# Layer 3 of a four-layer fp32 network in Strassen's form: folding, ranks and last product with seven block products, and weights turned earlier

## The chip, the cores and the metric

The kernel runs on one core of a Trainium2 chip. The metric is the device time of one execution in microseconds (us), median of several runs. A core has five engines that run their own instruction queues in order and wait for one another by semaphores: TensorE (PE, matrix products; PEld are its weight loads), VectorE (DVE), ScalarE (ACT), GpSimd (POOL) and SyncE (SP, which here issues transfers). TensorE writes its results to PSUM, eight banks of 2 KB for each of the 128 partitions; the other tiles lie in SBUF.

## What is computed

Four layers work on 1024 tokens of width 512, each adding its result to `x`. Everything is fp32. The change is in layer 3, and begins at the end of layer 2:

```python
# layer 3, first part (y = _L3_cond_ref(x)): base weights and gated low-rank experts
base = einsum('btd,od->bto', x, W)
logits = einsum('btd,ed->bte', x, Wr) + 5 * one_hot(language)
gates = softmax over the two largest logits, 0 elsewhere
y = base + 2.0 * einsum('bter,bte,eor->bto', einsum('btd,erd->bter', x, A), gates, B)
# layer 3, second part (_L3_ffn_ref(y)): 64 experts of rank 8, the best 16 gated
scores = einsum('bsr,er->bse', einsum('bsd,rd->bsr', y, Wq_w), keys)
gate = softmax over the 16 largest scores, 0 elsewhere
z = einsum('bsd,nd->bsn', y, A_w)            # 512 ranks, 8 for each expert
out = x + einsum('bsn,on->bso', z * gate, B_w) * 2.0
```

Layer 2 ends by adding to `x` a product with its weights `W2` and a gated low-rank delta.

## The kernel before

`x` lies in SBUF with the width on the partitions: four chunks of 128 (`DC`) by 1024 tokens. Tokens are worked in two halves (`g` = 0, 1) of four blocks of 128 (`HB`).

**Layers 0 to 2** fill the span up to about 1387 us; layer 2's attention is by far the longest. Several of their products are already in the form that the change brings to layer 3 (`gates_by_seven` L432, `Down` L570, `seven` L948): a product of 2x2 blocks with seven block products in place of eight, the sums of blocks made by VectorE or POOL.

**The end of layer 2** (`layer2`, L2026) runs, for each block of tokens, 16 products of 128x128 blocks into one PSUM bank (`product`, L1786, tile `h`), and leaves them there until `delta` (L1873) adds the low-rank part into the same bank, and VectorE adds the bank to `x` (L1882). Banks here carry the tags "st" (three of them), "av" (two) and "mm" (three). Blocks 0 to 2 lie in "st", 3 and 4 in "av", 5 to 7 in "mm". The routing between (L1800) is a chain on VectorE with one POOL all-reduce (L1812).

**Layer 3** (`layer3`, L2045) has a pool of eight banks of its own, which lies where the earlier banks lay. It never forms `y`. Instead it folds weights with weights:

- `weights_turned` (L1911) transposes on TensorE `base3` into `L3.W` (tile `W3p`, four banks), `wB3` into `wBT`, and `Wq3` into `wqT`; ScalarE copies each bank out (L1908).
- `fold_scores` (L1928) multiplies them with the keys: `kwp`, `fkp` (32 recorded matmuls of 64 columns) and `gkp`.
- `mids(g)` (L227, tile `midp_l`) are the products of `x` with the low-rank inputs, the router and the folded score weights; `route(g)` (L239) is a chain of some fifteen VectorE operations; `mix(g)` (L280) transposes the gated ranks (`midTp_l`) and ScalarE copies them to `midT_l` (L285).
- `fold_ranks` (L1943) makes `F` = W times A_w (tile `fp`, 16 matmuls of 512 columns) and, from `wBT`, `G` (tile `gp`).
- `scores(g)` (L1957) finishes the scores (`sc`) and picks the best 16 on VectorE: about 40 short operations.
- `ranks(g)` (L1992): for each block of tokens four matmuls of 512 columns with `F` and one with `G` into one bank (tile `z`); VectorE multiplies the bank by the gates (L2002).
- `turned(g)` (L2010) transposes the gated ranks (`zT`), ScalarE copies them to `zgT` (L2016).
- `last(g)` (L2018): 16 matmuls of 512 columns (tile `o`), VectorE adds each bank to `x` (L2023), SP sends it to HBM (L2024, 256 KB each).

In the trace each fp32 matmul of the program appears as two recorded ones.

**The order.** A planner orders each engine's instructions by the order in which the program names them and by the times at which it takes their inputs to be ready; it may put a later one ahead where an earlier one is not ready. Only those wrapped in `kept` are pinned, and layer 3's are not. VectorE's `sums_checked` (L742), for instance, is named between `turned(0)` and `last(0)` and runs at 1418 us. A tile with a tag takes the room of the last tile with that tag, once that is no longer used.

Of the kernel before, what the change touches and what calls it, by code (L numbers as in the profile page):

```python
# [10 lines left out]
F32 = mybir.dt.float32  # L11
# [6 lines left out]
P = 128  # L18
# [29 lines left out]
def forward(ctx: ExitStack, tc: tile.TileContext, a: dict, out: bass.AP):  # L48
# [615 lines left out]
    with psa:  # L664
# [53 lines left out]
        def bank(tag, shape, name):  # L718
            return ps_.tile(shape, F32, tag=tag, name=name, bufs=2 if tag == "av" else 3)

        def end_of(in_order):
            return ending(
                tc, a, out, x, ident, bias3, experts, late,
                lambda shape, name: ww.tile(shape, F32, tag="q7", name=name),
                lambda shape, name: ww.tile(shape, F32, tag="qs", name=name), chunks, mm, in_order,
            )

        y2, end = att.run(late, end_of, bank, lambda: sp.dma_start(kept, x))
# [28 lines left out]
    with tc.If(redo > 0):  # L757
        sp.dma_start(x, kept)
        y2 = attention_any(tc, a, x, ident, lens, kvrow, part, ww, wop, ypool, eps, rows, chunks, mm)
        with ExitStack() as c3:  # L760
            late = c3.enter_context(tc.tile_pool(name="late_a", bufs=1, side="right"))
            w3 = c3.enter_context(tc.tile_pool(name="w3_a", bufs=1))
            ex["sm"] = c3.enter_context(tc.tile_pool(name="sm3_a", bufs=2, side="right"))
            psp = c3.enter_context(tc.tile_pool(name="ps3_a", bufs=8, space=PSUM))

            def bank(tag, shape, name):
                return psp.tile(shape, F32, tag="mm", name=name)

            end = ending(
                tc, a, out, x, ident, bias3, experts, late,  # L770
                lambda shape, name: ww.tile(shape, F32, tag="q7", name=name),
                lambda shape, name: ww.tile(shape, F32, tag="qs", name=name), chunks, mm,
            )
            for _ in end.prepare(bank, lambda shape, name: late.tile(shape, F32, tag="oT", name=name)):
                pass
            end.load_w2()
            end.load_aw()
            end.shifted()
            end.open3(w3, ex["sm"])
            end.layer2(y2, bank)  # L780
            end.layer3(bank)
# [901 lines left out]
    return y2  # L1683


def ending(tc, a, out, x, ident, bias3, experts, early, tile_of_w2, tile_of_aw, chunks, mm, kept=lambda i: i):

# [7 lines left out]
    def half(g):  # L1697
        return slice(g * 512, (g + 1) * 512)
# [229 lines left out]
    def fold_scores(bank):  # L1928
# [11 lines left out]
            mm(ps, L3.wBT[:, o, :], kw[:, o, :], o == 0, o == DC - 1)  # L1940
        L3.GK = copied([P, NE], "gk3", ps)

    def fold_ranks(bank):  # L1943
        L3.F = L3.w3.tile([P, DC, D], F32, tag="F3", name="F3")
        for d in range(DC):
            ps = bank("mm", [P, D], f"fp_{d}")
            for o in range(DC):
                mm(ps, L3.W[:, o, d * P : (d + 1) * P], W["a"][:, o, :], o == 0, o == DC - 1)
            copied(None, None, ps, L3.F[:, d, :])
        ps = bank("mm", [P, D], "gp")  # L1950
        for o in range(DC):
            mm(ps, L3.wBT[:, o, :], W["a"][:, o, :], o == 0, o == DC - 1)
        L3.G = copied([P, D], "g3", ps)
# [35 lines left out]

    G3 = {}  # L1990

    def ranks(g, bank):  # L1992

        T = L3.steps[5]
        for i in range(HB):
            b = g * HB + i
            ps = bank("mm", [P, 512], f"z3_{b}")
            for c in range(DC):
                mm(ps, x[:, c, b * P : (b + 1) * P], L3.F[:, c, :], c == 0, False)
            mm(ps, T[g][:, i * P : (i + 1) * P], L3.G, False, True)  # L2000
            zg = L3.w3.tile([P, 512], F32, tag="zg", name=f"zg_{b}", bufs=4)
            dve.tensor_tensor(  # L2002
                zg.rearrange("p (e r) -> p e r", r=NR),
                ps.rearrange("p (e r) -> p e r", r=NR),
                gates[g][:, i, :].unsqueeze(2).to_broadcast([P, NE, NR]),
                ALU.mult,
            )
            G3[b] = zg

    def turned(g, bank):  # L2010
        for i in range(HB):
# [3 lines left out]
                pe.transpose(ps[:, c, :], G3[b][:, c * P : (c + 1) * P], ident)  # L2015
            act.copy(L3.zgT[:, :, b * P : (b + 1) * P], ps)  # L2016

    def last(g, bank):  # L2018
        for o in range(DC):
            ps = bank("mm", [P, 512], f"o3_{g}_{o}")  # L2020
            for c in range(DC):
                mm(ps, L3.Bw[:, c, o * P : (o + 1) * P], L3.zgT[:, c, half(g)], c == 0, c == DC - 1)
            dve.tensor_tensor(x[:, o, half(g)], ps, x[:, o, half(g)], ALU.add)  # L2023
            sp.dma_start(out[o * P : (o + 1) * P, half(g)], x[:, o, half(g)])  # L2024

    def layer2(y2, bank, held=lambda: None, do=range(NB)):  # L2026

# [12 lines left out]
        delta(0)  # L2040
        for b in range(HB + 1, NB):
            product(b, "mm", bank)
        delta(1)

    def layer3(bank, between=lambda: None):  # L2045
        mids, route, mix = L3.steps[:3]
# [1 line left out]
        def plain(shape, name):  # L2048
            return bank("mm", shape, name)

        weights_turned(bank)
        fold_scores(bank)
        mids(0, plain)
        route(0)
        fold_ranks(bank)
        mix(0, plain)
        scores(0, bank)
        mids(1, plain)
        route(1)
        ranks(0, bank)  # L2060
        mix(1, plain)
        scores(1, bank)
        turned(0, bank)
        between()
        last(0, bank)
        ranks(1, bank)
        turned(1, bank)
        last(1, bank)

    return SimpleNamespace(  # L2070
        prepare=prepare, load_w2=load_w2, load_aw=load_aw, turn=turn, low=low, anchors=anchors,
# [67 lines left out]
```

## Time and profile before

| | |
|---|---|
| median of three runs (1558.67 to 1561.76) | 1560.63 us |
| profiled execution | 1556.86 us, span 1555.1 us |
| TensorE busy | 1519.5 us (98% of the span) |
| VectorE / POOL / ScalarE busy | 66% / 53% / 35% |
| chain that ended last, by engine | TensorE 87%, VectorE 5%, transfers 3%, POOL 2% |
| mean granted TensorE clock | 0.995 |
| last deltas of layer 2 to the end of the span | 1431.4 to 1555.1 us |
| last addition ends; last transfer's data move | 1550.4 us; 1551.0 to 1552.5 us |

The span runs from the first to the last recorded instruction; the execution's own time has 1.8 us more. Matmuls overlap at their ends, so the duration of a group of matmuls is a little longer than the distance to the start of the next; the distance is what counts. Idle time of TensorE is printed in brackets, with what ended it.

### The profile page before, as it was taken

To read this page: it belongs to the slowest core of one execution; us is meant where nothing else is said; L and a number is where in the kernel's file an instruction comes from. 1 tells how busy PE (TensorE), PEld (TensorE's weight loads), DVE (VectorE), ACT (ScalarE), POOL (GpSimd) and SP (SyncE) were. 2 spreads that over 40 slices of the span, in tenths; PEclk is the share of its full clock that TensorE was granted. 3 is DMA by queue.
4 is the path that set the end of the run, shared out by engine and by line. 5 is a ranking of instruction groups with operands and counts; after the bars stand their busy time and mean duration, and the time that the engine had idled before them with its cause. 6 is when DMAs were issued, how large, how long until landed. Compare 5 with 4: busy or idle time off the path is not lost.

```text
span 1555.1 us, 18566 instructions
## 1 busy us (share of the span) xinstructions
PE 1519.5 (98%) x5991; PEld 928.9 (60%) x5991; DVE 1025.3 (66%) x1963; ACT 538.0 (35%) x1324; POOL 829.0 (53%) x842
## 2 busy tenths in 40 slices
PE   9999999989999999999999999999999999999998
PEld 7888886535555555556555556555555555568743
DVE  4666334477878776777877778777777878643141
ACT  1111110144445444445444445444445434321110
POOL 1341105285767777767777667777667777600000
PEclk9999999999999999999999999999999999999899
DMA  9111002154654544553454444456444435430000
GB/s 301 44 42 31 1 0 63 53 134 107 175 158 131 146 123 130 145 155 99 136 161 135 140 119 135 115 148 168 127 126 141 123 102 155 147 90 7 0 21 36
DMA packets 156682, 169.89 MB, mean 109 GB/s; under 512 B 54144, under 2 KB 127040, under 8 KB 156448
## 3 DMA queue, kind: packets, MB, share of 16 engines
q1 hardware_dynamic: 138144, 131.27, 29.7%
q0 software_dynamic: 17056, 36.49, 8.1%
q10 hardware_dynamic: 1376, 0.85, 0.2%
q8 instruction: 50, 0.82, 0.2%
q14 instruction: 56, 0.46, 0.1%
HBM read 113.89 MB, written 42.07 MB: 100 GB/s over the span
## 4 chain that ended last, share of the span: by engine, by line
PE 87%; DVE 5%; DMA 3%; POOL 2%; issue 1%; ACT 1%; SPq 0%; ACTq 0%; DVEq 0%; POOLq 0%
PE av L1177 17%; PE st L1126 16%; PE q_six L962 7%; PE g L362 7%; PE q_one L962 5%; PE q_five L962 5%; PE wo_two L962 5%; PE dn L362 5%; PE wo_six L962 3%; PE wo_one L962 3%; PE eo_l L53 2%; PE z L53 2%; PE h L1704 2%; PE o L53 2%; PE midp_l L53 1%
## 5 line engine op out<-in xcount | busy, mean ns | idle before, releaser
L905 POOL DMA_INDIRECT kn<-in_k_cache,kvrow_k x256 | 281.3, 1099 | 73.3 <-issue 66.3
L1177 PE MATMUL av<-pT,vals 128*128 128x512 f32 x640 | 300.1, 600 | 0.0
L905 POOL DMA_INDIRECT vals<-in_v_cache,kvrow_v x256 | 259.4, 1013 | 73.5 <-issue 41.8
L1130 ACT ACTIVATE pT<-st,hide 128x512 f32<-128x512 f32 x256 | 175.9, 687 | 328.7 <-PE st L1126 328.7
L1126 PE MATMUL st<-qT,kT 128*128 128x512 f32 x512 | 235.9, 593 | 2.9 <-DMA qT<-turned_new 2.8
L1051 POOL TENSOR_TENSOR vq<-q,txq 128x256 f32<-128x256 f32 x128 | 118.3, 954 | 174.8 <-ACT sqq L1035 122.5
L1177 PEld LDWEIGHTS av<-pT,vals 128*128 128x128 f32 x640 | 119.5, 191 | 144.9 <-issue 143.0
L1126 PEld LDWEIGHTS st<-qT,kT 128*128 128x128 f32 x512 | 96.7, 190 | 111.9 <-issue 105.2
L1146 DVE TENSOR_TENSOR part<-pT 128x512 f32<-128x512 f32 x128 | 88.4, 693 | 80.4 <-ACT pT L1130 80.4
L962 PE MATMUL q_one<-q,x 128*128 128x384 f32 x256 | 93.0, 486 | 0.0
L1162 DVE RECIPROCAL rr<-sum 128x256 f32<-128x256 f32 x32 | 56.2, 1756 | 41.3 <-PE sum L1155 41.3
L1035 ACT ACTIVATE sqq<-q 128x128 f32<-128x128 f32 x256 | 79.3, 310 | 11.3 <-DVE q L1011 4.6
L962 PEld LDWEIGHTS q_one<-q,x 128*128 128x128 f32 x256 | 48.5, 190 | 39.8 <-issue 14.3
L962 PE MATMUL q_six<-q_s,xs_all 128*128 128x384 f32 x192 | 69.8, 486 | 0.0
L962 PE MATMUL wo_one<-o,oT 128*128 128x256 f32 x256 | 65.7, 379 | 0.0
L1126 PE MATMUL st<-qT,kTn 128*128 128x512 f32 x128 | 65.4, 592 | 0.0
L1215 POOL TENSOR_TENSOR y<-y,uo 128x512 f32<-128x512 f32 x32 | 41.3, 1290 | 43.3 <-DVE y L1207 42.8
L1016 ACT COPY q<-q_one 128x256 f32<-128x256 f32 x32 | 11.9, 372 | 148.7 <-PE q_one L962 148.7
L962 PE MATMUL wo_two<-o_s,os 128*128 128x256 f32 x256 | 60.6, 380 | 2.5 <-DVE os L921 2.3
L1130 ACT ACTIVATE pT<-st,rs 128x512 f32<-128x512 f32 x64 | 44.0, 687 | 38.4 <-PE st L1126 38.3
L962 PEld LDWEIGHTS wo_one<-o,oT 128*128 128x128 f32 x256 | 48.6, 190 | 13.4 <-PE st L1126 0.4
L362 PE MATMUL g<-xs,ws 128*128 128x256 f32 (+1 forms) x240 | 55.2, 379 | 1.4 <-POOL ws L429 1.4
(396 smaller groups left out, 2693.5 us busy)
## 6 DMA issues: line engine op xcount, KB each, us to landing
turned_new<-qkt SPq DMA_DIRECT2D x126, 160.0 KB
turned_cached<-kt SPq DMA_DIRECT2D x128, 128.0 KB
kT<-turned_cached SPq DMA_DIRECT2D x32, 512.0 KB
qT<-turned_new SPq DMA_DIRECT2D x32, 512.0 KB
R<-R SPq DMA_DIRECT2D x96, 128.0 KB
q<-in_WqT SPq DMA_DIRECT2D x8, 1024.0 KB
o<-in_WoT SPq DMA_DIRECT2D x8, 1024.0 KB
kn<-in_k_cache,kvrow_k POOLq DMA_INDIRECT x256, 2.9
```

The lines of the kernel that those rows point to most:

```text
L53: pe.matmul(o, lhsT, rhs, start=start, stop=stop)
L362: pe.matmul(o, lhsT, rhs, start=start, stop=stop, skip_group_check=True)
L905: kept(pool.indirect_dma_start(out=d[:, c, :], out_offset=None, in_=kc if what == "k" else vc, in_offset=bass.IndirectOffsetOnAxis(ap=kvro ...
L962: kept(pe.matmul(o, l[:, c, :], r[:, c, :], start=start and c == 0, stop=c == 1, skip_group_check=True))
L1035: kept(act.activation(sq, S[n][m][:, j, i, :], AF.Square, accum_out=S[n]["ssq"][:, j, col : col + 1]))
L1051: kept(pool.tensor_tensor(to, t[:, b, :, hi : hi + 64], wx[:, b, lo : lo + 64].unsqueeze(2).to_broadcast(list(to.shape)), ALU.mult,))
L1126: kept(pe.matmul(ps, s["kT"][:, c, 4 * j : 4 * j + 4, :] if c < 4 else s["kn"][:, j], s["qT"][:, :, REP * j : REP * (j + 1), :].rearrange( ...
L1130: kept(act.activation(pT[:, c, :, :].rearrange("p i t -> p (i t)"), ps, AF.Exp, **(dict(bias=hide[:, b, c : c + 1]) if c < 4 else dict(bia ...
L1146: kept(dve.tensor_tensor(o, l, r, ALU.add))
L1162: kept(dve.reciprocal(r, S[n]["sum"]))
L1177: kept(pe.matmul(ps, v[:, c, :], pT[:, c, :, :].rearrange("p i t -> p (i t)"), start=c == 0, stop=c == NC - 1, skip_group_check=True,))
L1215: kept(pool.tensor_tensor(t, t, u.unsqueeze(1).to_broadcast([P, 2, HW]), ALU.add))
```

## The change

A block product C = A B with A and B cut into 2x2 blocks is made from seven products of blocks: P1 = a11 b11, then a12 b21, s1 t1, s2 t2, s3 t3, s4 b22 and a22 t4, where s1 to s4 are sums and differences of A's blocks and t1 to t4 of B's. One set (`Seven`) makes four outputs of 128 rows by 256 columns, in two banks, `even` and `odd`, of two outputs each. ScalarE copies P1 out; VectorE makes two further partial sums (`u`, and `p1` in two steps) while the matmuls go on, and the outputs but the first are a bank half plus one of these.

- `fold_ranks` makes `F` in two sets, `ranks` each half in two, `last` each half in two: ten sets. `G` is made in a function of its own, `fold_last`, named after `mix(0)`.
- POOL makes the sums of the left operands (`left_sums`): of `Bw` and `W` once, of `x` for each half. VectorE makes those of the right operands (`right_sums`): of `AwT`, `F` and `zgT`. Their tiles take the room of tags "y", "os", "o7", "q7" and "qs", whose earlier tiles are used no more by then.
- A gate is now multiplied onto a quarter of a pair of blocks at a time; outputs go out in 16 transfers of 128 KB.
- `weights_turned` is named in `layer2` ahead of the last deltas, `fold_scores` after them, both with "st" banks.
- In `layer3`, `turned(0)` stands before `scores(1)`; the first set of `last(0)` stands before `ranks(1)` and the second after it; in the second half both P1 are made before the other products.

The core of the diff:

```diff
+    def left_sums(a11, a12, a21, a22, t, by):
+        s1, s2, s3, s4 = (t[:, k] for k in range(4))
+        for o, l, r, op in (
+            (s1, a21, a22, ALU.add), (s2, s1, a11, ALU.subtract),
+            (s3, a11, a21, ALU.subtract), (s4, a12, s2, ALU.subtract),
+        ):
+            by.tensor_tensor(o, l, r, op)
+        return a11, a12, a22, s1, s2, s3, s4
+
+    def right_sums(b11, b12, b21, b22, t):
+        t1, t2, t3, t4 = (t[:, k] for k in range(4))
+        for o, l, r in ((t1, b12, b11), (t2, b22, t1), (t3, b22, b12), (t4, b21, t2)):
+            dve.tensor_tensor(o, l, r, ALU.subtract)
+        return b11, b21, b22, t1, t2, t3, t4
...
+    class Seven:
+        def __init__(self, name, bank, A, B):
+            self.A, self.B = A, B
+            self.even, self.odd = (bank("mm", [P, 2, 256], f"{name}_{i}") for i in range(2))
+            self.p1, self.u = (
+                L3.w3.tile([P, 256], F32, tag=f"seven_{n}", name=f"{n}_{name}", bufs=2) for n in ("p", "u")
+            )
+            self.c = {(0, 0): (self.even[:, 0], None), (0, 1): (self.odd[:, 1], self.u),
+                      (1, 0): (self.even[:, 1], self.u), (1, 1): (self.odd[:, 0], self.p1)}
+        def into(self, o, l, r, start=False):
+            for c in range(2):
+                mmq(o, l[:, c, :], r[:, c, :], start and c == 0, False)
+        def begin(self):
+            self.into(self.even[:, 0], self.A[0], self.B[0], True)
+            act.copy(self.p1, self.even[:, 0])
+        def go_on(self):
...
+            self.into(odd[:, 1], s1, t1, True)
+            self.into(odd[:, 0], s2, t2)
+            dve.tensor_tensor(u, odd[:, 0], p1, ALU.add)
+            dve.tensor_tensor(p1, odd[:, 1], p1, ALU.add)
+            self.into(even[:, 1], s3, t3)
+            dve.tensor_tensor(p1, even[:, 1], p1, ALU.add)
+            self.into(odd[:, 1], s4, b22)
+            self.into(even[:, 0], a12, b21)
+            self.into(even[:, 1], a22, t4)
...
+    def weights_summed():
+        ts = room("y", [P, 2, 4, 2, 256], "sums3")
+        S["a"] = right_sums(*right(W["a"], 0), ts[:, 0])
+        S["f"] = ts[:, 1]
+        tw = room("os", [P, 2, 4, 2, P], "Bws")
+        S["b"] = [left_sums(*left(L3.Bw, k), tw[:, k], pool) for k in range(2)]
+
     def fold_ranks(bank):
         L3.F = L3.w3.tile([P, DC, D], F32, tag="F3", name="F3")
-        for d in range(DC):
-            ps = bank("mm", [P, D], f"fp_{d}")
-            for o in range(DC):
-                mm(ps, L3.W[:, o, d * P : (d + 1) * P], W["a"][:, o, :], o == 0, o == DC - 1)
-            copied(None, None, ps, L3.F[:, d, :])
+        tw = room("o7", [P, 2, 4, 2, P], "W3s")
+        for k in range(2):
+            f = Seven(f"fp_{k}", bank, left_sums(*left(L3.W, k), tw[:, k], pool), S["a"])
+            f.begin()
+            f.go_on()
+            for (i, j), (ps, more) in f.c.items():
+                t = L3.F[:, 2 * k + i, j * 256 : (j + 1) * 256]
+                if more is None:
+                    act.copy(t, ps)
+                else:
+                    dve.tensor_tensor(t, ps, more, ALU.add)
+        S["f"] = right_sums(*right(L3.F, 0), S["f"])
+
+    def fold_last(bank):
         ps = bank("mm", [P, D], "gp")
...
+    def rank_sums(g):
+        t = room("o7", [P, 2, 4, 2, P], f"xs3_{g}")
+        S["x", g] = [left_sums(*left(x, HB // 2 * g + k), t[:, k], pool) for k in range(HB // 2)]
+
     def ranks(g, bank):
...
+        for k in range(HB // 2):
+            f = Seven(f"z3_{g}_{k}", bank, S["x", g][k], S["f"])
+            f.begin()
+            f.go_on()
+            for i in range(2):
...
+                for j in range(2):
+                    ps, more = f.c[i, j]
+                    part = slice(j * 256, (j + 1) * 256)
+                    mmq(ps, T[g][:, b * P : (b + 1) * P], L3.G[:, part], False, True)
+                    if more is not None:
+                        dve.tensor_tensor(zg[:, part], ps, more, ALU.add)
+                        ps = zg[:, part]
+                    dve.tensor_tensor(
+                        zg[:, part].rearrange("p (e r) -> p e r", r=NR),
+                        ps.rearrange("p (e r) -> p e r", r=NR),
+                        gates[g][:, b, j * NG : (j + 1) * NG].unsqueeze(2).to_broadcast([P, NG, NR]),
+                        ALU.mult,
+                    )
...
+    def last(g, k):
+        f = S["o", g, k]
+        f.go_on()
+        for (i, j), (ps, more) in reversed(f.c.items()):
...
+            if more is not None:
+                dve.tensor_tensor(t, t, more, ALU.add)
+        for ij in ((1, 1), (0, 1), (0, 0), (1, 0)):
...
+            dve.tensor_tensor(t, ps, t, ALU.add)
+            sp.dma_start(out[o * P : (o + 1) * P, tok], t)
@@ layer2
+        def free(tag, shape, name):
+            return bank("st", shape, name)
+
+        weights_turned(free)
         delta(1)
+        fold_scores(free)
@@ layer3
-        weights_turned(bank)
-        fold_scores(bank)
+        weights_summed()
         mids(0, plain)
         route(0)
         fold_ranks(bank)
         mix(0, plain)
+        fold_last(bank)
         scores(0, bank)
         mids(1, plain)
+        rank_sums(0)
         route(1)
         ranks(0, bank)
         mix(1, plain)
+        turned(0, bank)
         scores(1, bank)
-        turned(0, bank)
         between()
-        last(0, bank)
+        last_sums(0, tile_of_w2)
+        last_begun(0, 0, bank)
+        last(0, 0)
+        rank_sums(1)
         ranks(1, bank)
+        last_begun(0, 1, bank)
+        last(0, 1)
         turned(1, bank)
-        last(1, bank)
+        S["z", 1] = right(L3.zgT, 1)
+        for k in range(2):
+            last_begun(1, k, bank)
+        last_sums(1, tile_of_aw)
+        for k in range(2):
+            S["o", 1, k].B = S["z", 1]
+        last(1, 0)
+        last(1, 1)
```

`last_sums(g, tile)` makes the right sums of `zgT`'s half, `last_begun(g, k)` makes the set and its P1.

## The prediction, made before the changed kernel was run

> **What bounds the kernel now.** I read the page first (engine totals), then the chain of work that ended last over the tail, then TensorE's timeline from 1430 us to the end, then the granted clock microsecond by microsecond where that timeline ran slow, and last the rows that price the added operations.
>
> The page: TensorE is busy for nearly the whole span; VectorE (DVE) and GpSimd (POOL) have room.
>
> ```profile
> PE 1519.5 (98%) x5991; PEld 928.9 (60%) x5991; DVE 1025.3 (66%) x1963; ACT 538.0 (35%) x1324; POOL 829.0 (53%) x842
> ```
>
> TensorE's timeline (start, duration, line, tiles, count, idle before and its releaser). Read the idle brackets, and the two `midp_l` rows: the same 32 matmuls take 7.96 us once and 5.63 us the second time.
>
> ```profile
> 1431.41 1.17 PE L1704 MATMUL h<-zp,Bm 32*128 32x128 f32 x32
> 1432.52 0.66 PE L1917 MATMUL W3p<-ident,base 128*128 128x128 f32 x4
> 1435.15 1.53 PE L1917 MATMUL W3p<-ident,base 128*128 128x128 f32 x12 [1.97 <-DVE x L1882]
> ...
> 1438.37 1.10 PE L53 MATMUL kwp<-keysT,wq3T 16*128 16x64 f32 x8 [0.82 <-ACT wq3T L1908]
> 1439.94 5.65 PE L53 MATMUL fkp<-kw,W 128*128 128x64 f32 x32 [0.46 <-ACT kw L1908]
> ...
> 1447.08 7.96 PE L53 MATMUL midp_l<-wmr,x 128*128 128x200 f32 x32
> 1454.88 13.90 PE L53 MATMUL fp<-AwT,W 128*128 128x512 f32 x32
> ...
> 1473.37 1.10 PE L53 MATMUL sc<-gk,midT_l 128*128 128x64 f32 x8 [0.73 <-ACT midT_l L285]
> 1474.31 5.63 PE L53 MATMUL midp_l<-wmr,x 128*128 128x200 f32 x32
> ...
> 1498.22 1.10 PE L53 MATMUL sc<-gk,midT_l 128*128 128x64 f32 x8 [0.68 <-ACT midT_l L285]
> ...
> 1501.91 14.00 PE L53 MATMUL o<-zgT,BwT 128*128 128x512 f32 x32 [0.83 <-ACT zgT L2016]
> ```
>
> The windows of one microsecond (busy of each engine, then the granted TensorE clock, DMA share, GB/s): the clock falls to half at 1441.6 us and returns at 1451.8 us.
>
> ```profile
> 1440.00:1441.00 1.00, 1.00 (x10) 1.00 (x10) 0.00 (x0) 0.00 (x0) 0.00 (x0) 1.00 0.00 0
> 1441.00:1442.00 1.00, 1.00 (x10) 1.00 (x9) 0.00 (x0) 0.00 (x0) 0.00 (x0) 0.78 0.00 0
> 1442.00:1443.00 1.00, 1.00 (x6) 1.00 (x6) 0.00 (x0) 0.00 (x0) 0.00 (x0) 0.50 0.00 0
> 1451.00:1452.00 1.00, 1.00 (x5) 1.00 (x4) 0.00 (x0) 0.00 (x0) 0.00 (x0) 0.60 0.00 0
> ```
>
> So layer 3 (1432.5 us on) is bound by TensorE's own streaming, plus 5.5 us of short waits for a PSUM eviction, plus one dip of the clock.
>
> [...]the dip lasts 10.2 us[...] and follows 7.4 us (1432.5 to 1439.9) of transposes, waits and the small `kwp`. [...]an fp32 two-tensor operation [...]here 0.42 us for 256 columns and 0.69 us for 512. [...]L479 (both inputs in SBUF, POOL summing beside it) shows 0.675 us where L477 (one input in PSUM) shows 0.414 us at the same size.[...]
>
> **The change, part by part.** Prices of the new form: four recorded 128x256 matmuls, one block product, pass in 0.86 us (eight in 1.73 us between starts below); two VectorE additions in a row take 0.94 us; POOL sums 0.75 to 0.90 us.
>
> ```profile
> 1394.40 1.89 PE L962 MATMUL wo_two<-o_s,os 128*128 128x256 f32 x8
> 1396.13 1.03 PE L962 MATMUL wo_six<-o_s,os 128*128 128x256 f32 x4
> ...
> 180.34 0.42 DVE L597 TENSOR_TENSOR du_dn<-dn,dp_dn 128x256 f32<-128x256 f32 x1 [2.67 <-issue]
> 180.86 0.42 DVE L598 TENSOR_TENSOR dp_dn<-dn,dp_dn 128x256 f32<-128x256 f32 x1
> ...
> L429 POOL TENSOR_TENSOR ws<-wg,ws 128x256 f32<-128x256 f32 x8 | 7.2, 902 | 0.0
> L429 POOL TENSOR_TENSOR ws<-wu 128x256 f32<-128x256 f32 x8 | 6.0, 749 | 81.1 <-DMA wu<-in_WuT 81.1
> ```
>
> (a) Seven products for eight: 2 block sets in the folding, 4 in the ranks, 4 in the last product. A set has two K-chunks, so eight products are 16 matmuls of 256 columns (the same streaming as before's eight of 512) and seven are 14; the two that go are four recorded ones, 0.86 us. 10 x 0.86 = 8.6 us less.
>
> (b) The turned weights ahead of the last deltas, in "st" banks free since the first deltas were added (by 1423.1 us): the 1.97 us wait for the last deltas' additions goes (fold_scores, 5 us of TensorE work, covers their 2.48 us), and the last deltas cover the copies that `kwp` waited 0.82 us for. 2.8 us less. Six ACT copies at 0.5 us against six groups of transposes at 0.44 us, on three banks: no wait of note. The 0.46 us for `kw` stays.
>
> (c) Reordering: fold_last (3.45 us) stands between mix(0) and its scores, turned(0) (1.8 us) between mix(1) and its scores, scores(1) between turned(0) and its product: 0.73 + 0.68 + 0.83 = 2.2 us less. The 0.83 us before the second half's product stays.
>
> (d) The clock. At full clock `fkp` goes at 0.1 us each (window 1440 to 1441): 3.2 us, not 5.6; `gkp` 0.8, not 1.7; `midp_l` 5.5, not 7.75 (to the next start). 5.6 us are lost to the dip. Afterwards the waits before it are gone: 2.6 us of transposes, 1.1 us of deltas, 1.1 us of `kwp`, 0.46 us of wait, then `fkp`, about half dense (64 columns[...], 53 ns of each 100).[...] I take it that the clock stays: 5.6 us less; the bounds are 0 and 5.6.
>
> (e) Added waits inside a block set. `s4*b22` goes into the half bank that the second addition reads; u and p1 end 0.94 + 0.1 us after s2t2, s3t3 lasts 0.86: about 0.2 us, times 10 = 2.0.[...] Bounds 0 (the planner fills it) and 5.
>
> (f) VectorE crowding. Layer 3's VectorE work after 1447 us goes from about 31 us to 67 (fold 12 additions, ranks 40, last 40, all at 0.42 = 38.6; two sets of sums and F's, 12 at 0.69 = 8.3; routing and scores 20). Between the first half's ranks and its first block of outputs: routing 4.1, ranks 8.4, scores(1) 5.6, sums 2.8, outputs 4.2 = 25 us against 25.6 us of TensorE. Behind each u or p1 stands TensorE's `s4*b22`; behind the sums of zgT its s1t1. The order on VectorE is the planner's; routing steps depend on each other, which lets an addition in between, but the 20 short steps of scores(1) do not. I take 2.6 us; bounds 0 and 10.
>
> (g) POOL: four times eight sums, 6.7 us each time. Bw's start when the tile of Wo's sums is free (1399.8) and may push the routing's all-reduce (1408.3) by under a microsecond; its result was ready 2.5 us before TensorE used it. W3's run from about 1435 us, used from 1447. Those of x wait for the tile (released in the folding's last products), with 12.9 us of cover for the first four. AwT's sums (2.8 us, VectorE) fall into its idle time before 1432. All at nothing; without cover a set of four costs 3.3 us.
>
> (h) The end: last addition 0.42 for 0.69, last transfer 128 KB for 256, but four close together and 16 issues for 8 on SP (0.33 us each). 0.3 us less; bounds -0.5 and 1.
>
> Sum: 8.6 + 2.8 + 2.2 + 5.6 - 2.4 - 2.6 + 0.3 = 14.5 us. The profiled execution took 1556.86 us (span 1555.1 and 1.8 around it), 3.8 us under the median of 1560.63; I carry the difference over: 1560.6 - 14.5 = 1546.1 us, some 1542.4 in a profile.
>
> **Rivals.**
> Clock dips anyway (0.23): `fkp` is still half dense[...]. Minus 5.6: 1551.7 us.
> VectorE's queue binds (0.12): for it, 25 us against 25.6; against it, dependent steps leave gaps. Folding waits for routing(0) to end (2.4 us), ranks(0) for routing(1) (2.4), the last product for scores(1) (5.6): 10.4 in place of 2.6, so 1553.9 us.
> The front does not move (0.04): the turned weights get banks that the last deltas hold; (b) and (d) vanish: 1554.5 us.
> Slower (0.05): POOL's sums set the pace. With d us each, W3's sums lose 8d - 18.1, those of x 8d - 20.8 and 8d - 21.6 (eight sums less their cover up to the second set's s1t1: from the copies of W at 1435.1 to 1453.2; from the tile's release through 12.9 us to the first set's s1t1 and one rank set of 7.9; likewise, 0.8 more, in the second half); 24d - 60.5 reaches the 17.6 us that turn the sign at d = 3.25 us, four times the rows above; at 3.4 us it gives 1567 us.
> The likeliest keeps 0.56.
>
> **Numbers.** 0.2% is 3.1 us, about what a measurement here can tell: faster means under 1557.5, slower over 1563.7. Faster 0.88 (nearly all of the likeliest and the dip, most of the next two), same 0.06 (a dip and a blocked VectorE together, 1559.5), slower 0.06. The likeliest alone spans 1542 to 1550 by most of the bounds of (e), (f) and (h) (all of their good ends at once would be 1540.1); going up to 1555.5 takes in the dip and most of the blocked VectorE.
>
> **What would show it.** `fp`, `z` and `o` in 128x256 with 28, 56 and 56 matmuls by program (twice that recorded); no wait of `W3p`; no dip of the granted clock near the end and both `midp_l` groups near 5.6 us; waits of these products for VectorE under 5 us in sum. Wrong if the clock falls again, if one such wait exceeds 2 us, or if a product waits for POOL.

## The result, and the profile after

The changed kernel took 1546.15 us (median of six executions, 1540.74 to 1548.98) beside 1561.1 us for the kernel before: a ratio of 0.9907 [0.9893, 0.9921]. Timed again beside later experiments it took 1548.7 us beside 1560.99, 0.9924 [0.9908, 0.994]. It is faster by 12 to 15 us, 0.8 to 0.9%; the prediction was 1546.1 us. The agreement is better than the reasons for it, as the trace shows.

The profiled execution took 1545.81 us (span 1544.0), against 1556.86 (1555.1). The page's engine totals, of the kernel after:

```profile
PE 1512.5 (98%) x6127; PEld 953.0 (62%) x6127; DVE 1062.8 (69%) x2055; ACT 540.4 (35%) x1332; POOL 850.9 (55%) x874
```

TensorE's timeline of the opening of layer 3, after (start, duration, line, tiles, count, idle before and its releaser):

```profile
1430.89 1.94 PE L1923 MATMUL W3p<-ident,base 128*128 128x128 f32 x16
1432.67 0.65 PE L1927 MATMUL wB3p<-ident,wB 128*128 128x128 f32 x4
1433.15 0.60 PE L1931 MATMUL wq3p<-ident,Wq 128*16 128x128 f32 x4
1433.68 1.17 PE L1710 MATMUL h<-zp,Bm 32*128 32x128 f32 x32
1434.67 1.00 PE L53 MATMUL kwp<-keysT,wq3T 16*128 16x64 f32 x8
1436.13 5.28 PE L53 MATMUL fkp<-kw,W 128*128 128x64 f32 x32 [0.46 <-ACT kw L1914]
1441.21 1.91 PE L53 MATMUL gkp<-kw,wB3T 128*128 128x64 f32 x8
1442.92 6.65 PE L53 MATMUL midp_l<-wmr,x 128*128 128x200 f32 x32
```

The waits of 1.97 us (`W3p`) and 0.82 us (`kwp`) are gone; only the 0.46 us ahead of `fkp` stays. But `fkp`, `gkp` and `midp_l` are again slow: the clock still falls. The one-microsecond windows after (busy of PE, PEld, DVE, ACT, POOL, then the granted clock, DMA share, GB/s):

```profile
1438.00:1439.00 1.00, 1.00 (x8) 1.00 (x7) 0.00 (x0) 0.00 (x0) 1.00 (x2) 0.57 0.00 0
1439.00:1440.00 1.00, 1.00 (x7) 1.00 (x6) 0.00 (x0) 0.00 (x0) 0.85 (x2) 0.50 0.00 0
1444.00:1445.00 1.00, 1.00 (x4) 1.00 (x4) 0.00 (x0) 0.00 (x0) 0.00 (x0) 0.51 0.00 0
1445.00:1446.00 1.00, 1.00 (x7) 1.00 (x7) 0.00 (x0) 0.00 (x0) 0.00 (x0) 1.00 0.00 0
```

Half clock from about 1438.1 to 1445.0 us: 6.8 us, where before it was 10.2. In the products that follow, the same timeline shows the waits that the seven-product form brought in, and that the second `midp_l` runs at full clock (5.63):

```profile
1453.62 1.10 PE L1710 MATMUL fp<-AwT,W3s 128*128 128x256 f32 x4 [0.17 <-DVE s_l L267]
1466.07 1.00 PE L53 MATMUL sc<-gk,midT_l 128*128 128x64 f32 x8
1466.90 5.63 PE L53 MATMUL midp_l<-wmr,x 128*128 128x200 f32 x32
1491.13 0.41 PE L2113 MATMUL zT<-ident,zg 128*128 128x128 f32 x2 [0.47 <-DVE zg L2100]
1491.90 0.44 PE L2113 MATMUL zT<-ident,zg 128*128 128x128 f32 x2 [0.36 <-DVE zg L2100]
1494.29 1.13 PE L1710 MATMUL o<-zs,Bws 128*128 128x256 f32 x4 [0.20 <-DVE zs L1964]
1498.17 2.13 PE L1710 MATMUL o<-zs,Bws 128*128 128x256 f32 x8 [0.15 <-DVE zs L1964]
1534.08 1.13 PE L1710 MATMUL o<-zgT,Bws 128*128 128x256 f32 x4 [0.18 <-DVE p_o L2002]
```

All brackets of this part (one more of 0.17 us is not shown) add up to 1.7 us, none for POOL; `sc` no longer waits.

To see where time goes, cut the end of every trace at three places: the **opening** (start of layer 2's product 5, the first product behind the first deltas, to the first fold-rank product), the **products** (from there to TensorE's last), and the **end** (from there to the span's end).

| us | opening | products | end | sum |
|---|---|---|---|---|
| before | 34.39 | 94.78 | 5.44 | 134.61 |
| after | 29.33 | 87.54 | 7.06 | 123.93 |
| after, profiled again | 31.00 | 87.54 | 5.72 | 124.26 |

The opening and the products are good to 0.02 us, the other two columns to 0.05.

### The profile page after: what moved, and what is told of

It is laid out like the page before. It is cut to its first block, busy times and chain, and to the rows that moved or that the text cites. A ratio compares the mean times of both kernels' runs of the same rounds, so it can differ in the third digit from the quotient of the medians.

```text
span 1544.0 us, 19040 instructions
## 1 busy us (share of the span) xinstructions
PE 1512.5 (98%) x6127; PEld 953.0 (62%) x6127; DVE 1062.8 (69%) x2055; ACT 540.4 (35%) x1332; POOL 850.9 (55%) x874
## 4 chain that ended last, share of the span: by engine, by line
PE 88%; DVE 5%; DMA 2%; POOL 2%; issue 1%; ACT 1%; ACTq 0%; DVEq 0%; SPq 0%; POOLq 0%
PE av L1181 17%; PE st L1130 17%; PE q_six L966 8%; PE g L362 7%; PE q_one L966 5%; PE q_five L966 5%; PE wo_two L966 5%; PE dn L362 5%; PE wo_six L966 3%; PE wo_one L966 3%; PE eo_l L53 2%; PE h L1710 2%; PE z L1710 2%; PE midp_l L53 1%; PE o L1710 1%; PE sum L1159 1%
## 5 line engine op out<-in xcount | busy, mean ns | idle before, releaser
L429 POOL TENSOR_TENSOR ws<-wu 128x256 f32<-128x256 f32 (+1 forms) x9 | 6.4, 712 | 90.7 <-DMA wu<-in_WuT 90.7
```

## Experiments

Beside some of them the kernel before took 1575.12 us (turning alone, seven products alone, the pinned order, the first spread) or 1578.46 us (the wait removed, `kwp` thrice), on other chips; the difference lies ahead of the part studied here. So times are compared by their ratio to the kernel before, and traces by the three parts.

**1. Each part alone.** The weights turned earlier alone: the diff's lines in `layer2` and `layer3` put into the kernel before. The seven products alone: the changed kernel with

```diff
-        weights_turned(free)
         delta(1)
-        fold_scores(free)
...
     def layer3(bank, between=lambda: None):
+        weights_turned(bank)
+        fold_scores(bank)
```

> The kernel before with one part of the change alone: the base weights turned ahead of layer 2's last deltas and the folded scores behind them, in the three banks with the tag st; all products plain. Theory A (the seven-product form earns its 8.6 us, the rest is the front): the stretch from the last product of layer 2 to the first product of the folding shrinks by about 5 us (23.5 to 18.5, as in the profile after), so some 1556 us and a ratio of 0.997 to before. Theory B (the front and the clock earn most, the handoffs eat the seven-product form): 10 us or more, under 1551 us. If the clock does not dip in most executions, 8.4 us: 1552.5.

> The changed kernel with the turned weights and folded scores back at the start of layer 3; the seven-product form stays. Theory A: loses the 5 us of the front, some 1551 us (ratio 0.9935 to before), with the wait of W3p for the last deltas' additions (2 us) and a dip of the clock of some 10 us back in the profile. Theory B: 1556 us or more.

Measured: turning alone 0.9958 [0.9943, 0.9974], parts 29.34, 94.79 and 5.80; seven products alone 0.9949 [0.993, 0.9969], parts 35.81, 87.52 and 7.81. The gains, 0.42% and 0.51%, add up to the whole change's 0.93%. The first is more and the second less than Theory A had it (0.997 and 0.9935), by no more than the intervals allow. Each part acts in its own stretch to within 0.02 us of its value in the whole change, except that the clock's fall in the opening differs from trace to trace (in the second, which keeps the wait of 1.97 us for `W3p`, the clock fell once more right behind that wait).

**2. The planner's freedom taken away in layer 3.** Every TensorE instruction of layer 3 pinned to the order in which it is named:

```diff
-        pe.matmul(o, lhsT, rhs, start=start, stop=stop)
+        pin(tc, pe.matmul(o, lhsT, rhs, start=start, stop=stop))
```

> The changed kernel with TensorE's instructions of layer 3 pinned to the order in which the program names them. Theory E (the waits of 5.0 us that were priced for handoffs and for VectorE's queue exist, and the planner hid them by putting other products into them): waits of TensorE for VectorE of about 5 us, at s4*b22 of each set (0.2 us), behind the routing (up to 2.4 us) and behind scores(1), time about 1550 us. Rival F (VectorE is simply in time): waits as after the change, under 2 us, and 1546 us.

Measured: 0.9969 [0.9956, 0.9982]; parts 26.05, 95.50, 5.83. The products take 7.96 us more than in the changed kernel, with the same matmuls. The waits of TensorE over this part (total us, times, longest):

```profile
PE o L1717 <- DVE zs L1971: 2.9, 2, 2.7
PE z L1717 <- DVE p_z L2009: 0.8, 3, 0.3
PE z L1717 <- DVE s_l L274: 0.6, 1, 0.6
PE fp L1717 <- DVE s_l L274: 0.6, 1, 0.6
```

So the handoffs inside the sets and the wait for the sums of `zgT` are real; in the changed kernel the planner fills many of them with matmuls of other sets. Not all of the 7.96 us are waits, though: right behind the longest one the clock fell for 3.41 us (from 1512.0 us), which cost 1.7.

```profile
1512.00:1513.00 1.00, 1.00 (x3) 0.83 (x3) 1.00 (x4) 0.00 (x0) 0.00 (x0) 0.50 0.00 0
```

With it the products take 0.7 us longer than they did before the change, without it they would take about 1 us less: nearly the whole gain of the eighth product is gone. This trace is that of the fastest of 22 executions (1563.97 us; their median is 1570.36) and had no fall of the clock in the opening, so its parts can't be set against the ratio of the medians.

**3. The turning spread between layer 2's products**, so that layer 3 does not open with all its small products in a row (first alone, then also with the last four outputs issued in turn by SP and ACT):

```diff
+        product(HB + 1, "mm", bank)
         weights_turned(free)
+        product(HB + 2, "mm", bank)
+        fold_scores(free)
+        product(HB + 3, "mm", bank)
         delta(1)
-        fold_scores(free)
```

> The changed kernel with the turned weights, the folded scores and the last deltas spread between layer 2's last three blocks of products, so that transposes and 64-column matmuls never fill 6.8 us alone. Theory C[...]: no dip near the end, mean clock 0.998 or more, the 3.8 us that the dip costs after the change and the 0.46 us wait for kw gone: about 1542 us, ratio 0.988. Rival D (the 64-column matmuls bring the dip by themselves, or it is due to something else at that point): the dip is there, shifted, and the time stays within 1.5 us of 1546.

> The changed kernel with the turning of W3 put between layer 2's products 5, 6 and 7, so that layer 3 opens with no stretch of small matmuls alone, and with the last four outputs issued in turn from two queues instead of one. Theory A: no fall of the clock, first fold product at 3.6 to 3.7 us, from product 5 to the end 118.5 to 119.5 us; a time 3 us (0.2%) below the changed kernel beside it and executions within 2 us of each other. If the end is set by SP's issues, the end after VectorE's last result falls from 5.5 to 7.0 us to about 5.0. If the end is set by the last transfer and its completion alone, it stays at 5.0 to 5.5 whatever the queue. Rival C: the turning's place matters nothing, and the two kernels agree within 0.1% but for the end.

> The changed kernel itself, timed beside the next kernel. Its time was 0.9907 of the kernel before; its profile there held the clock at half for 6.8 us between the first fold product and the first middle product, and its executions reached from 1540.7 to 1549.0 us. Theory A (the shortened front still falls under the clock's limit in some executions, and the seven products save what was priced): 0.990 to 0.992 of before, executions spread over some 6 us or more, and the part from the start of layer 2's product 5 to the end between 120.5 us (no fall of the clock) and 125 us (a fall of two or three windows). Theory C (the first profile's fall was a single accident and the changed kernel normally has none): below 0.989, spread under 3 us, 120.5 us in that part.

Measured: 0.990 [0.9876, 0.9925] for the first, not the 0.988 expected; the clock did not fall in the opening, as expected, but other falls, ahead of the part studied here, kept the mean clock at 0.994. The second 1544.52 us (1540.34 to 1548.13), 0.9895 [0.9876, 0.9914], beside the changed kernel's 1548.7 (1546.44 to 1552.01), 0.9924: 4.2 us apart, but the ranges overlap, and its executions did not lie within 2 us of each other as expected. The openings took 25.92 us in both traces, with no fall of the clock there; the changed kernel, profiled again, had a fall of 10.24 us (an opening of 31.00). The six executions each say the same: the clock granted over the whole span was 0.995 to 0.999 (mean 0.9963) in the second kernel and 0.992 to 0.997 (mean 0.9937) in the changed one, and 0.0026 of the span are 4.0 us. TensorE's timeline of the second:

```profile
1432.69 1.10 PE L53 MATMUL kwp<-keysT,wq3T 16*128 16x64 f32 x8
1433.72 0.94 PE L1710 MATMUL h<-y2T,WT 128*128 128x128 f32 x6
1434.49 3.68 PE L53 MATMUL fkp<-kw,W 128*128 128x64 f32 x32
1438.02 1.06 PE L53 MATMUL gkp<-kw,wB3T 128*128 128x64 f32 x8
1438.91 3.12 PE L1710 MATMUL h<-y2T,WT 128*128 128x128 f32 x26
```

`fkp` takes 3.68 us, not 5.28, and the wait for `kw` is covered by six matmuls of a product. The edit does two things at once, though: it breaks up the run of small products, and it takes away the wait.

**4. Which of the two lowers the clock.** The changed kernel with one group of small products done three times into the same place (transposes of W3; then `fkp`; then `kwp`, each by `list(range(DC)) * 3`), and, the other way, with only the wait removed: `Wq` turned first and `kwp` put ahead of the last deltas, all small products still in one run.

```diff
         weights_turned(free)
+        fold_keys(free)
         delta(1)
         fold_scores(free)
```

> The changed kernel with each of W3's sixteen transposes done three times into the same place, so that the stretch of small matmuls ahead of layer 3 is 32 transposes longer: 3.9 us at full clock. Theory A (a long enough stretch of small, light matmuls lowers the clock): the clock falls to half for at least as long as in the profile of the changed kernel, and earlier in the stretch; from product 5 to layer 3's first fold ranks the time grows from 29.3 us by more than the transposes' 3.9 us, to 35 to 39 us. Theory C (the fall does not depend on the stretch): the time grows by 3.9 us to 30 to 33.3 us.

> The changed kernel with the products that fold the keys into the weights (fkp, 32 matmuls of 128 by 64) done three times into the same place: 7.2 us more of them at the full clock. Tripling the transposes did not lengthen the fall of the clock, which began 1.3 to 3 us into fkp each time. Theory L (the run of 64-column products is what lowers the clock): the clock falls within 4 us of fkp's start and stays down to fkp's end, so that fkp takes 16 to 20 us instead of 10.9, and the loss is 7 us or more. Theory M (the fall has a length of its own, two or three windows, whatever keeps running): the loss stays at 3.4 to 5.1 us and fkp takes 14 to 16 us.

> The changed kernel with the eight matmuls of kwp (16 rows, 64 columns) done three times into the same place: 2.0 us more of them at the full clock, the wait of 0.46 us kept. Theory N (16-row products count as little activity beside the wait): the fall comes within 3.4 us of the wait's end, whatever the phase of the windows, so fkp and what follows lose 3.4 to 5.1 us, and from product 5 to the first fold ranks it is 31.5 to 33.5 us. Theory N without the part on rows (only the stop counts): no surer than before, 28.1 to 33.5 us.

> The changed kernel with the small product of the keys (kwp) put ahead of layer 2's last deltas, and Wq turned before W3, so that the first fold product no longer waits 0.46 us for ScalarE's copy of kwp; all the small products stay in one run. In the traces so far the clock goes down by windows of 3.4 us, and each fall at this place began at the end of a window that held most of kwp or this wait together with the start of fkp, and none where fkp ran on for 11 us without a wait. Theory N (a stop of TensorE, with the 16-row product beside it, is what pulls a window under the limit): no fall, fkp 3.6 to 3.7 us, 25.4 to 25.9 us from product 5 to the first fold ranks, and a time 3 to 5 us below that of the changed kernel, near 0.990 of before or under. Theory L (the run of small products itself): the fall stays, fkp takes 4.6 us or more, 28 us or more from product 5 to the fold ranks.

Measured openings: transposes thrice 32.77 us, with a fall of 6.83 us like the changed kernel's; `fkp` thrice 33.20, with none; `kwp` thrice 32.76, with one of 10.24; the wait removed 25.59, with none. TensorE's timeline at `fkp`, of the kernel with `fkp` thrice:

```profile
1438.57 10.93 PE L53 MATMUL fkp<-kw,W 128*128 128x64 f32 x96 [0.46 <-ACT kw L1914]
```

Of the kernel with `kwp` thrice, where `fkp` starts at full and ends at half clock:

```profile
1456.21 2.79 PE L53 MATMUL kwp<-keysT,wq3T 16*128 16x64 f32 x24
1459.46 6.50 PE L53 MATMUL fkp<-kw,W 128*128 128x64 f32 x32 [0.46 <-ACT kw L1914]
```

Of the kernel with the wait removed, where `fkp` follows the last deltas without a bracket:

```profile
1459.11 1.11 PE L1710 MATMUL h<-zp,Bm 32*128 32x128 f32 x29
1460.15 3.79 PE L53 MATMUL fkp<-kw,W 128*128 128x64 f32 x32
```

The eleven microseconds of 64-column matmuls at full clock (the first of these) refute both expectations for that run: the small products alone did not lower the clock, and neither did three times as many transposes by themselves. The 32.76 us of `kwp` thrice lie in both of the ranges given for it, so that time does not tell its 16 rows from the stop. More is seen from where the falls lie. In the traces they lasted 3.41, 6.83 or 10.24 us (but for the last one of a trace, which its end cuts off): once, twice or three times 3.413. Within a trace they start a whole multiple of 3.413 us apart (after: 345.9, 1366.5 and 1438.15 us, 299.0 and 21.0 times it), so the other falls of a trace say where its stretches of 3.413 us, here called windows, begin. The window that holds the wait for `kw`, or most of it, then holds:

| | `kwp` | wait | `fkp` | clock then |
|---|---|---|---|---|
| before (with 0.23 us of the wait for `wq3T`) | 1.1 us | 0.46 | 1.6 | falls |
| after | 0.9 | 0.46 | 2.0 | falls |
| after, again | 1.0 | 0.46 | 1.7 | falls |
| turning alone | 0.95 | 0.46 | 2.0 | falls |
| seven products alone (with 0.67 us of the wait for `wq3T`) | 1.1 | 0.46 | 1.2 | falls |
| transposes thrice | 0.4 | 0.46 | 2.5 | falls |
| `kwp` thrice | 2.3 | 0.46 | 0.7 | falls |
| experiment 5 below | 0.2 | 0.46 | 2.75 | falls |
| pinned order | 0 | 0.32 | 3.1 | stays |
| `fkp` thrice | 0.03 | 0.46 | 2.9 | stays |
| spread (three traces), wait removed | | none | | stays |

(The starts are good to 0.1 us.) All eight windows with the whole wait and 0.2 us or more of the 16-row `kwp` were followed by a fall; the two with the wait and hardly any `kwp` were not. In these two, however, the window begins inside the wait (pinned order) or 0.03 us ahead of it, so they do not tell whether the 16-row matmuls count for little, or whether the whole wait must lie in one window. Nor does the length of a stop decide alone. In the kernel before, the window from 1431.3 to 1434.7 us held 1.56 us of the wait for `W3p`, beside layer 2's last deltas and four transposes, and no fall followed:

```profile
1433.00:1434.00 1.00, 0.17 (x2) 0.00 (x0) 1.00 (x3) 0.58 (x1) 0.00 (x0) 1.00 0.00 0
1434.00:1435.00 1.00, 0.00 (x0) 0.00 (x0) 1.00 (x2) 0.00 (x0) 0.00 (x0) 1.00 0.00 0
```

Its four stops of 0.68 to 0.83 us in the part of the products brought none either. The whole 1.97 us in one window (seven products alone, behind 0.2 us of deltas and 1.25 us of transposes) did. So in these traces it was the stop together with what else the window held; by which measure, these runs do not show.

Where the windows cut this stretch differs from trace to trace: `fkp` began 1.4 us into one in the first profile of the changed kernel and 1.7 in the second, 0.3 to 2.75 over all traces with the wait. In the eight falls here the clock stayed low behind each window with only `fkp`, `gkp` and up to 1.4 us of `midp_l`; behind one with 2.0 us of `midp_l` or more it came back. A low window full of transposes (seven products alone, 1452.0 to 1455.4 us) brought it back too.

With the wait removed there is one trace, and in it `kwp` and `fkp` lay in different windows. The clocks of whole executions speak for more than this one: 0.994 to 0.996 in the six with the wait removed, 0.989 to 0.992 in the seven with `kwp` thrice, and 0.990 to 0.993 in the kernel before beside them. They take in falls elsewhere, so a rare one here is not excluded. The times agree: with the wait removed the ratio is 0.9903 [0.9882, 0.9924], with `kwp` thrice 0.9954 [0.9935, 0.9973]; single executions of 1549.84 (transposes thrice) and 1550.66 us (`fkp` thrice) stand beside 1560.99 and 1562.91.

**5. GpSimd's sums of x made by VectorE.**

```diff
-        S["x", g] = [left_sums(*left(x, HB // 2 * g + k), t[:, k], pool) for k in range(HB // 2)]
+        S["x", g] = [left_sums(*left(x, HB // 2 * g + k), t[:, k], dve) for k in range(HB // 2)]
```

> The changed kernel with the sums of x for the rank products (16 of 128 by 256) made on VectorE instead of GpSimd. Theory A (GpSimd's sums cost the path nothing themselves but slow VectorE's 256-column operations beside them from 0.42 to 0.8 us, and so make the wait of 0.8 us of the transposes of zg): VectorE's busy time grows by some 6.7 us; its operations on sums and zg go back to 0.42 and 0.69 us; the wait of the transposes for zg falls below 0.4 us, but products wait for the sums of x that stand in VectorE's queue instead, 0 to 1.5 us each; the total within 1.5 us of the changed kernel. Rival D (GpSimd's sums are late and products wait for them): the total falls by more than 1.5 us.

Measured: 1547.42 us, 0.9908 [0.9888, 0.9927], not to be told from the changed kernel beside it by time; the opening (29.36, with a fall) and the end (7.48) are as disturbed as the changed kernel's. But the products take 86.18 us, not 87.54. VectorE's groups from 1460 to 1492 us (count | busy us, mean ns | idle before), of the changed kernel:

```profile
L2100 DVE TENSOR_TENSOR zg<-zg,gate 128x256 f32<-128x256 f32 x6 | 3.8, 661 | 0.1
L1964 DVE TENSOR_TENSOR sums<-F,sums 128x512 f32<-128x512 f32 x2 | 2.0, 1016 | 0.1
```

The same groups with the sums of x on VectorE:

```profile
L2100 DVE TENSOR_TENSOR zg<-zg,gate 128x256 f32<-128x256 f32 x5 | 2.0, 421 | 0.0
L1964 DVE TENSOR_TENSOR sums<-F,sums 128x512 f32<-128x512 f32 x2 | 1.4, 686 | 0.0
```

The operations with both inputs in SBUF go from 0.66 to 0.42 us and from 1.02 to 0.69, and the transposes' wait for `zg` is gone, although VectorE has 16 operations more. Those of `zg` that read PSUM took 0.42 either way. The 0.66 is a mean of unlike operations: three beside GpSimd's sums took 0.79, 0.98 and 0.94 us, the other three 0.42. VectorE's timeline of the changed kernel:

```profile
1488.17 0.42 DVE L2098 TENSOR_TENSOR zg<-z,u_z 128x256 f32<-128x256 f32 x1
1488.63 0.79 DVE L2100 TENSOR_TENSOR zg<-zg,gate 128x256 f32<-128x256 f32 x1
1490.01 1.84 DVE L2100 TENSOR_TENSOR zg<-zg,gate 128x256 f32<-128x256 f32 x2
```

The first of these rows, with one input in PSUM, lay beside such a sum as well. GpSimd's sums were longer there too: 0.73 us otherwise, and 0.9 to 1.2 beside such operations. The kernel before shows the same at L479, whose mean of 0.675 us the prediction gives: 0.42 in nine with no more than 0.1 us of a sum beside them, 0.94 to 0.96 in eight with one beside them nearly throughout, 0.81 in one.

**6. The three improvements joined** (spread, two queues, sums on VectorE).

> Three edits together: the turning of W3 between layer 2's products, the last four outputs from two queues, and the sums of x for the rank products on VectorE. If they are independent: no fall of the clock at layer 3's opening (first fold product 3.6 to 3.7 us), no wait of the transposes for zg, 117.7 us from product 5 to the end (119.05 less the 1.3 that the sums on VectorE took off), a ratio of 0.988 to 0.990 to the kernel before. If the saving of the sums on VectorE and that of the turning's place are the same time, or if VectorE is then late elsewhere: 119 us or more.

Measured: 1541.82 us (1539.64 to 1544.06), 0.9872 [0.9849, 0.9895]; parts 25.92, 86.18, 5.93, sum 118.03. The opening and the products add up exactly; the end is 0.3 us longer than the 5.60 of experiment 3's second kernel. This is the fastest of all that ran: 21 us under the kernel before (1562.91).

## Why the prediction came out, step by step

The profile was expected at "some 1542.4" and was 1545.81: the change saved 11.05 us there, not 14.5. The carrying over of 3.8 us from the profiled execution to the median then erred the other way: the kernel after was profiled 0.3 us under its median. By luck two errors of some 3.5 us cancel in the 1546.1. The median lies even inside the 1542 to 1550 us of the likeliest case, which has no dip, so the range holding says nothing about the dip. By its steps:

**(a) Seven products, -8.6: right.** By the distances between starts, a recorded matmul of 256 columns costs 0.2159 us, of 512 columns 0.4292. At such prices (64, 128 and 200 columns 0.112, 0.109 and 0.169) the streaming of the products' part is 90.5 us before and 82.4 after: -8.2. Two matmuls of 256 columns cost a little more than one of 512.

**(b) The waits of `W3p` and `kwp`, -2.8: right.** Both brackets are gone, and turning alone shortened the opening by 5.05 us, of which the shorter fall explains 1.7; that leaves 3.3, the two brackets and the restarts of TensorE that brackets leave out.

**(c) Reordering, -2.2: too small; (e) and (f), +5.0: right in sum.** What the products' part took beyond its streaming (and the 0.16 us by which the last matmul's record outlasts its price) is 4.1 us before and 5.0 after, so these steps together cost 0.9 us instead of 2.8. Before, the starts behind the four waits for `midT_l` and `zgT` lie 3.9 us later than streaming alone explains. A bracket leaves out TensorE's slower restart, 0.16 us at each and 0.10 more at the second matmul behind the two waits for `zgT`; and the fourth wait (0.83), which (c) left standing and the prediction's 5.5 us of waits left out, went too. After, the handoffs inside sets (e) cost 2.2 us, 0.3 to 0.45 at six sets and 0.1 or nothing at those where the planner had another product to put in: the price per set (0.2) was half the true one, the sum (2.4) right; 0.4 of that sum, for the rank-to-rank matmuls, was an estimate that no trace of before showed. VectorE's crowding (f) cost 2.2 us, all between `ranks(0)` and the first outputs, where the prediction had put it, for 2.6.

**(d) The clock, -5.6: the step that failed.** In the profile 1.7 us came, and in a second profile of the same kernel nothing; by the prediction's own sign ("wrong if the clock falls again") it was wrong here. The size was nearly right: 10.24 us at half clock lose 5.1, and with no fall the opening took 26.05 us (pinned order), where 34.39 - 3.3 - 5.1 is 26.0. What failed is the step from the shorter waits to a clock that stays: it was the author's estimate, and nothing in the trace of before showed that it was enough. After, the window ahead of the fall held 0.9 us of `kwp`, 0.46 of wait and 2.0 of `fkp`, and the clock fell. One full window ahead of a stop did not prevent a fall either: in the trace of the seven products alone it fell behind a window with 1.97 us of stop, though the window ahead of that was full of products. A run of 64-column matmuls passed (10.93 us at full clock); the 0.46 us wait, which (b) left standing as a small loss, stood in the window ahead of each of the eight falls tabled in experiment 4, and in the four traces without it none came. The 53 ns for the streaming of an `fkp` hold as an estimate: by the difference between 256 and 512 columns (0.2159 and 0.4292 us), 64 columns stream for 53 ns, half of the distance between starts (0.112 us). The rival "clock dips anyway", with 0.23 of the chance, named `fkp`'s density, which 10.93 us of it at full clock do not bear out; yet it fits the traces better than the forecast did, though with a shorter fall (3.4 or 5.1 us of loss for its 5.6).

In the trace of before, the window ahead of the fall (1438.1 to 1441.6 us) held only 0.7 us of stops, and none of the transposes. Nor did transposes by themselves lower the clock: a window wholly within the tripled transposes (1433.7 to 1437.1 us in that trace) brought no fall, and the low window full of transposes in experiment 4 was followed by the full clock.

**(g) POOL at nothing: wrong by 1.4 us.** No product waited for POOL, as predicted, and the slower rival (3.25 us per sum) had no hold: the sums took 0.7 to 0.9 us in the mean. But they slowed VectorE, which (f) then paid for: 87.54 - 86.18 = 1.36 us. The price was in the prediction's own text (0.675 us at L479 for 0.414 at L477), and was not used.

**(h) The end, -0.3: too good.** It was 1.6 us longer in the profile. One of SP's issues took 1.39 us there, the others some 0.4. The timeline of SP's last issues, after (the last row is two):

```profile
1535.91 0.33 SPq L2139 DMA_DIRECT2D out<-x  x1
1536.34 1.39 SPq L2139 DMA_DIRECT2D out<-x  x1
1537.82 0.88 SPq L2139 DMA_DIRECT2D out<-x  x2
```

The same kernel's second profile has an end of 5.72 us and no such issue. But the slow issue does not explain the longer end: the traces of the pinned order and of `kwp` thrice have issues of 1.64 and 1.29 us and ends of 5.83 and 5.57, and the last issue began 0.56 us behind VectorE's last addition in the first profile and 0.52 in the second. What differs is when the last packet of the outputs had moved, 3.86 us behind that addition in the first and 2.50 in the second; the cause stays open. The ends with one queue were 5.6 to 5.83 us in six of the ten traces with the new outputs and 6.3 to 7.8 in four; with two queues 5.60 and 5.93. The old outputs had 5.44 (before) and 5.80 (turning alone). So (h) is about nothing and sometimes +2; that two queues prevent it isn't settled by two traces.

The steps add up. In the profile the products are 7.2 us shorter, the opening is 5.1 us shorter and the end 1.6 us longer: 10.7 of the 11.05 us. What is left lies ahead of the part studied here.

**The other rivals.** VectorE's queue doesn't bind (the longest wait for it is 0.47 us), the front did move, and the slower one ended with (g).

## What to carry to other kernels

Where TensorE streams nearly all the time, price a change by the distances between starts, not by the brackets of idle time, and separate what differs between executions of one kernel (here the clock's fall, 6.83 and 10.24 us in two profiles, and the end, 7.06 and 5.72) from what the edit does: a second profile of the same kernel shows which is which. Look for a short stop of TensorE amid small matmuls; moving independent matmuls into it, or the work that it waits for ahead, can be worth far more than the stop (here 3.4 to 5.1 us for 0.46). Sums put on GpSimd cost the products no wait here, but VectorE's operations beside them took up to twice as long (0.8 to 1.0 us for 0.42), and the products 1.36 us more.

## What was not expected of the hardware

- A stop of 0.46 us, with 0.2 to 2.3 us of 16-row matmuls in the same 3.41 us window, was followed in eight traces of eight by two or three windows of half clock: 3.4 to 5.1 us lost. 10.93 us of 64-column matmuls behind such a stop, in a window that began 0.03 us ahead of the stop, ran at full clock, and so did what followed 1.56 us of stop in a window with transposes and deltas.
- In all eight of these falls a window of 64-column matmuls at half clock was followed by half clock again, though 10.93 us of them at full clock brought no fall. A window with 2.0 us or more of 200-column matmuls was followed by the full clock, and so, once, was one full of transposes (1452.0 to 1455.4 us, seven products alone).
- An fp32 operation of VectorE with both inputs in SBUF took 0.8 to 1.0 us beside GpSimd's sums instead of 0.42 (256 columns), and up to 1.27 instead of 0.69 (512); with one input in PSUM it took 0.42 beside them. Giving VectorE GpSimd's work as well made the products 1.4 us shorter.
- The same last transfers ended 1.4 us later in one execution than in another, with the issues no later.
